# Typed neighbour sums on one core: two nodes per counting slot, counts as bytes of 16-bit integers, and 480 counted chunks instead of 464

## The chip, the cores and the metric

The kernel runs on 1 core of one Trainium2 chip. A core has TensorE (PE, matrix products into PSUM; PEld in the profile is its weight load), VectorE (DVE), ScalarE (ACT), GpSimd (POOL) and SyncE (SP, which here only issues DMAs). The metric is the device time in microseconds, the median of the runs shown; lower is better. Before the change it is 1467.21 us (3 runs, 1465.16 to 1470.11).

## The reference

There are 12,500 nodes with 128 features, and 200,000 edges with a source node, a destination node and one of 4 types. The edges are sorted by destination, and the destinations are drawn as 12500 u² with u uniform, so that low nodes have many edges and high nodes few.

```
h = relu(layernorm(x))                      # 12500 x 128
msgs = sum_i where(type == i, h[src] @ W[i] + b[i], 0)    # 200000 x 128
out = x + segment_sum(msgs, dst, 12500)
```

The sum over edges can be taken before the product with W: for every destination and every type, add up the rows h[src], multiply the four sums by the four W, and add each b as often as its type occurs.

## The kernel before

The 200,000 edges are 1563 chunks of 128. A constant, C0 = 464, splits them. The first C0 chunks (destinations with many edges) go the counted way, the other TM = 1099 the gathered way. Both run at once in one program order.

*The node table.* In the first eight groups of chunks (RAW = 8) the kernel also normalises all nodes and writes h to DRAM (`htab`) as three bf16 parts whose sum is h. These groups gather rows of x itself; later ones gather rows of `htab`.

*The gathered way.* A group has G = 16 chunks; the last four groups have 12, 8, 4 and 3. For each chunk POOL issues one indirect DMA (L403) that fetches 128 rows. DVE makes a one-hot of destination and type (L424), PE sums the rows with it (L461, three products for the three parts), ACT evicts the sums (L468), PE multiplies them by W (L475), and DVE adds the result into a ring of destinations (L487). Buffers `hm` hold 5 x 8 chunks, so POOL can be 40 chunks ahead of PE. When destinations are complete, `put_out` takes four tiles of 128 nodes from the ring, PE transposes them (L509), DVE adds x (L512) and SP writes them out.

*The counted way.* For the first ND destinations the kernel doesn't fetch rows. It counts, for each destination, how many of its edges come from each source with each type, and multiplies `htab` by the counts. A *slot* is a column of up to 128 edges of one destination; `make_slots` builds the slots in the head of the kernel: `loT` and `hkT` hold, for each edge of a slot, the source's low part (0 to 127) and its high part combined with the type (1 to 392, 0 for none). A destination with over 128 edges has several slots, its levels; two levels share a *virtual* node. `count` makes two one-hots per slot on DVE (L737 with 128 columns, L738 with 392), multiplies them on PE (L742: a 128 x 392 table of counts in PSUM, a second level being added to the first), and ACT evicts the table of each virtual node as one byte of fp8 per count into `counts` (L745), with the sum of each row as accumulator output (`both`), which serves a check of the largest count. `multiply` then takes a batch of up to 92 virtual nodes (VBMAX), loads `htab` with 25 DMAs on SP (L763, `hs`, 5 buffers), and runs 98 x 3 products of 128 x 128 with up to 368 columns of counts (L766) into one PSUM tile, `pa`. It is evicted (L776), multiplied by W (L779) and added to `acc` (L784).

*The order.* `dense_work` is a generator that alternates the counting of one batch with the multiplication of the batch before it, in step with the share of each that is done. `pace` spreads it over the groups: it counts PE columns, and lets each group from RAW to `last` have the same sum of gathered and counted columns. The place of each instruction in its engine's queue is therefore fixed when the program is built; the engines meet through semaphores. After `last`, what is left of the counted work is issued at once, then come the remaining groups and the output of `acc`. At the end `check_all` sums the checks; if `flag` is set, a slow loop computes everything again.

With C0 = 464 there are ND = 1144 counted destinations, 1336 slots and 1180 virtual nodes in 15 batches (23, 46, eleven of 92, 53, 46), and 67 full groups.

Of the kernel before, what the change touches and what calls it, by code (L numbers as in the profile page):

```python
# [31 lines left out]
F32 = mybir.dt.float32  # L35
BF16 = mybir.dt.bfloat16
F16 = mybir.dt.float16
F8 = mybir.dt.float8e4
I32 = mybir.dt.int32
AF = mybir.ActivationFunctionType  # L40
ALU = mybir.AluOpType
AX = mybir.AxisListType
# [4 lines left out]
P = 128  # L47
# [4 lines left out]
WIN = 32  # L52
RAW = 8
ROOM = 12
C0 = 464
VBMAX = 92
MANY = 16
HB = 4
# [9 lines left out]
def kernel(  # L68
# [47 lines left out]
    virtual = [(k, d) for k in range(0, len(levels), 2) for d in range(levels[k])]  # L116

    virtual = virtual[ND - 2 * VBMAX : ND] + virtual[: ND - 2 * VBMAX] + virtual[ND:]
    VB = VBMAX
    sizes_of = [VB // 4, VB // 2]  # L120
    left = len(virtual) - sum(sizes_of) - VB // 2
    sizes_of += [VB] * (left // VB) + ([left % VB] if left % VB else []) + [VB // 2]
    batches = [virtual[sum(sizes_of[:i]) :][:n] for i, n in enumerate(sizes_of)]
    NB = NW * NT


# [427 lines left out]
    def check_all():  # L554

        low = const.tile([P, BM], F32, name="low")
        step = const.tile([P, BM], F32, name="step")
        nc.vector.memset(low, 0.0)
        for (ja, jb, _), i in zip(flushes, goes):
            if starts[i] + sizes[i] < TM:  # L560
                nc.vector.tensor_scalar(
                    step, rowf, starts[i] + sizes[i] - 0.5, (jb - ja) * float(P), ALU.is_gt, ALU.mult
                )
                nc.vector.tensor_add(low, low, step)
        bad = const.tile([P, 5], F32, name="bad")
# [10 lines left out]
        many = const.tile([P, 2], F32, name="many")  # L576
        nc.vector.tensor_reduce(many[:, 0:1], bad, AX.X, ALU.add)
        nc.vector.tensor_copy(many[:, 1:2], seen)
        pb = x_ps.tile([P, 2], F32, name="pt")
        nc.tensor.matmul(pb, ones, many, start=True, stop=True)  # L580
        sums_ok = const.tile([P, 2], F32, name="sums_ok")
        nc.vector.tensor_single_scalar(sums_ok[:, 0:1], pb[:, 0:1], 0.5, op=ALU.is_gt)
        nc.vector.tensor_single_scalar(sums_ok[:, 1:2], pb[:, 1:2], 3.0 * E0, op=ALU.not_equal)
        nc.vector.tensor_reduce(flag, sums_ok, AX.X, ALU.max)


# [12 lines left out]
    def make_slots(dix):  # L599
# [79 lines left out]
        def unpack(a, z):  # L679
            n = z - a  # L680
            hk = dix.tile([P, 512], I32, name="hk")
            nc.vector.tensor_single_scalar(hk[:, :n], packed[:, a:z], 7, op=ALU.arith_shift_right)
            nc.vector.tensor_copy(hkT[:, a:z], hk[:, :n])
            nc.vector.scalar_tensor_tensor(
                loT[:, a:z], hkT[:, a:z], float(-P), packed[:, a:z], op0=ALU.mult, op1=ALU.add
            )

            nc.vector.tensor_single_scalar(hk[:, :n], hk[:, :n], NT - 1, op=ALU.bitwise_and)
            ohs = []
            for t in range(NT):  # L690
                is_t = dix.tile([P, 512], BF16, name="is_t", bufs=NT)
# [32 lines left out]

    def count(vs, counts):
        todo = []
        for i, (k, d) in enumerate(vs):
            todo.append((i, starts_of[k] + d, True, not (k + 1 < len(levels) and d < levels[k + 1])))
            if not todo[-1][3]:
                todo.append((i, starts_of[k + 1] + d, False, True))  # L730
        both = sdp.tile([P, VB], F32, name="both", bufs=2)
        for s0 in range(0, len(todo), OB):
            part = todo[s0 : s0 + OB]
            o1 = ohp.tile([P, OB, P], BF16, name="o1")
            o2 = ohp.tile([P, OB, NB], BF16, name="o2")
            for k, (i, s, first, last) in enumerate(part):
                nc.vector.tensor_scalar(o1[:, k, :], iota_b, loT[:, s : s + 1], None, ALU.is_equal)  # L737
                nc.vector.tensor_scalar(o2[:, k, :], iota_n, hkT[:, s : s + 1], None, ALU.is_equal)  # L738
            for k, (i, s, first, last) in enumerate(part):
                if first:  # L740
                    pb = x_ps.tile([P, NB], F32, name="pt")
                nc.tensor.matmul(pb, o1[:, k, :], o2[:, k, :], start=first, stop=last)  # L742
                if last:

                    nc.scalar.activation(  # L745
                        counts[:, :, i * NT : (i + 1) * NT],
                        pb.rearrange("p (b t) -> p b t", t=NT),
                        AF.Copy,
                        accum_out=both[:, i : i + 1],
                        saturate=True,  # L750
                    )
                yield (s0 + k + 1) / len(todo)
        top = sdp.tile([P, 1], F32, name="top")
        nc.vector.tensor_reduce(top, both[:, : len(vs)], AX.X, ALU.max)
        nc.vector.tensor_max(most, most, top)

    def multiply(vs, counts):
        nv = len(vs)
        pa = a_ps.tile([P, VB * NT], F32, name="pa")
        for j0 in range(0, NW, HB):  # L760
            j1 = min(j0 + HB, NW)
# [10 lines left out]
                    )  # L772
            if j1 < NW:
                yield j1 / NW
        sd = sdp.tile([P, VB, NT], F32, name="sd")
        nc.scalar.copy(sd[:, :nv].rearrange("p v t -> p (v t)"), pa[:, : nv * NT])  # L776
        py = y_ps.tile([P, VB], F32, name="py")
        for t in range(NT):
            nc.tensor.matmul(py[:, :nv], wsb[:, t, :], sd[:, :nv, t], start=(t == 0), stop=(t == NT - 1))  # L779
        i = 0  # L780
        while i < nv:
            k, d = vs[i]
            n = next((m for m in range(1, nv - i) if vs[i + m] != (k, d + m)), nv - i)
            nc.vector.tensor_tensor(acc[:, d : d + n], acc[:, d : d + n], py[:, i : i + n], ALU.add)  # L784
# [7 lines left out]

    def pace(gi, part):

        last = FULL - 2
        if gi >= last:
            return 2.0
        own = [columns(i) for i in range(RAW, last)]
# [2 lines left out]
        return ((n + part) * a_group - sum(own[:n]) - part * own[n]) / dense_columns()  # L801

    def dense_columns():
        return NS * float(NB) + len(virtual) * NW * 3.0 * NT

    def dense_work():

# [5 lines left out]
        for vs in batches + [None]:  # L813
            steps = {}
            now = None
            if vs:
                now = vs, dense.tile([P, NW, VB * NT], F8, name="counts")
                slots = sum(1 + (k + 1 < len(levels) and d < levels[k + 1]) for k, d in vs)
                steps[count(*now)] = slots * a_slot
# [12 lines left out]
            before = now  # L832

    seen = const.tile([P, 1], F32, name="seen")
    slots = mid.enter_context(tc.tile_pool(name="slots", bufs=1, side="right"))
    loT = slots.tile([P, NS], F32, name="loT")
    hkT = slots.tile([P, NS], F32, name="hkT")
    building = ExitStack()
    dix = building.enter_context(tc.tile_pool(name="dix", bufs=1, side="right"))
    to_slots = make_slots(dix)  # L840
# [5 lines left out]
    for gi, (t0, g) in enumerate(zip(starts, sizes)):  # L846
# [85 lines left out]
        if gi == RAW - 1:  # L932
# [11 lines left out]
            most = sdp.tile([P, 1], F32, name="most")  # L944
            nc.vector.memset(most, 0.0)
            work = dense_work()
        for (ja, jb, _), i in zip(flushes, goes):
            if i == gi:
# [135 lines left out]
```

## Time and profile before

| | before |
|---|---|
| median of 3 runs | 1467.21 us |
| the profiled execution, its time / span | 1466.72 / 1465.0 us |
| granted TensorE clock, mean | 0.95 |
| PE, weight load busy | 1305.8, 866.6 us |
| DVE, ACT, POOL busy | 1055.8, 860.7, 1078.9 us |
| DMA | 282.11 MB, mean 193 GB/s |
| gathers: from `htab`, from x | 971, 128 |

Busy time is the union of the times in which an engine had an instruction in work. Instructions on PE, DVE and ACT overlap their successors, so the mean duration of one is longer than its share of the engine; the trace also has every start, and start-to-start times tell what one costs. A line of a group of instructions gives line, engine, operation, output <- inputs, shapes and count, then busy time and mean ns of one, then the idle time of the engine just before them with what ended it. A line of waits gives the engine and line that waited, what ended the wait, the total in us, how many, and the longest. A line of the chain of waits gives start, length, and what.

### The profile page before, as it was taken

To read this page: it belongs to the slowest core of one execution; us is meant where nothing else is said; L and a number is where in the kernel's file an instruction comes from. 1 tells how busy PE (TensorE), PEld (TensorE's weight loads), DVE (VectorE), ACT (ScalarE), POOL (GpSimd) and SP (SyncE) were. 2 spreads that over 40 slices of the span, in tenths; PEclk is the share of its full clock that TensorE was granted. 3 is DMA by queue.
4 is the path that set the end of the run, shared out by engine and by line. 5 is a ranking of instruction groups with operands and counts; after the bars stand their busy time and mean duration, and the time that the engine had idled before them with its cause. 6 is when DMAs were issued, how large, how long until landed. Compare 5 with 4: busy or idle time off the path is not lost.

```text
span 1465.0 us, 32946 instructions
## 1 busy us (share of the span) xinstructions
PE 1305.8 (89%) x10222; PEld 866.6 (59%) x10222; DVE 1055.8 (72%) x5728; ACT 860.7 (59%) x3026; POOL 1078.9 (74%) x1109
## 2 busy tenths in 40 slices
PE   1566787998999999999999999999999999999964
PEld 0444455765666556666666666666666666677743
DVE  8796878879889877677675786757787676677233
ACT  7776447867545566566655666646766665445010
POOL 7777775677677767777777777777777777777773
PEclk9995768999999999999999999999999999999977
DMA  7643247975566567676676767776676667777841
GB/s 214 181 138 115 89 149 245 299 231 173 154 193 176 165 183 204 190 225 200 202 205 196 210 186 207 199 200 201 192 209 193 190 194 212 216 237 252 304 121 54
DMA packets 141833, 282.11 MB, mean 193 GB/s; under 512 B 26995, under 2 KB 74661, under 8 KB 141653
## 3 DMA queue, kind: packets, MB, share of 16 engines
q1 hardware_dynamic: 90949, 176.07, 38.3%
q0 software_dynamic: 50704, 103.91, 26.3%
q8 instruction: 80, 1.31, 0.3%
q14 instruction: 100, 0.82, 0.2%
HBM read 263.84 MB, written 16.03 MB: 191 GB/s over the span
## 4 chain that ended last, share of the span: by engine, by line
PE 70%; DVE 11%; ACT 4%; DMA 3%; POOL 2%; issue 2%; DVEq 0%; ACTq 0%; POOLq 0%
PE pa L766 35%; PE pt L742 13%; PE py L475 9%; PE ps L461 8%; ACT counts L745 3%; DVE o L738 3%; DVE o L737 2%; POOL hm L403 2%; DVE ring L487 2%; DMA hs<-htab 2%; DVE oh L424 2%; DMA hm<-htab,srcT 1%; PE ps L444 1%; PE ps L446 1%; PE py L779 1%
## 5 line engine op out<-in xcount | busy, mean ns | idle before, releaser
L403 POOL DMA_INDIRECT hm<-htab,srcT x971 | 947.0, 975 | 322.4 <-issue 266.9
L766 PE MATMUL pa<-counts,hs 128*128 128x368 fp8e4 (+3 forms) x4410 | 713.2, 299 | 7.2 <-DMA hs<-htab 6.4
L745 ACT ACTIVATE counts<-pt 128x392 fp8e4<-128x392 f32 x1180 | 574.7, 519 | 169.7 <-PE pt L742 165.8
L766 PEld LDWEIGHTS <-hs 128*128 128x128 bf16 x4410 | 404.3, 99 | 232.4 <-issue 31.7
L738 DVE TENSOR_SCALAR o<-iota_n,hkT 128x392 bf16<-128x392 f16 x1336 | 450.3, 337 | 0.0
L737 DVE TENSOR_SCALAR o<-iota_b,loT 128x128 bf16<-128x128 bf16 x1336 | 346.8, 260 | 128.5 <-PE pt L742 126.7
L742 PE MATMUL pt<-o,o 128*128 128x392 bf16 x1336 | 368.0, 333 | 11.4 <-ACT counts L745 3.9
L745 ACT ACTIVATION_READ_ACCUMULATOR counts<-pt 128x1 f32 x1180 | 268.7, 228 | 0.0
L487 DVE TENSOR_TENSOR ring<-ring,py 128x16 f32 (+4 forms) x1072 | 187.3, 175 | 106.8 <-PE py L475 89.8
L468 ACT COPY sb<-ps 128x320 f32<-128x320 f32 (+4 forms) x275 | 115.8, 424 | 234.1 <-PE ps L461 210.0
L424 DVE TENSOR_SCALAR oh<-iota_b,keyT 128x64 bf16<-128x64 bf16 (+4 forms) x971 | 179.2, 265 | 90.1 <-PE ps L461 88.2
L461 PE MATMUL ps<-oh,hm 128*128 128x80 bf16 (+4 forms) x2913 | 160.0, 202 | 20.9 <-DMA hm<-htab,srcT 19.8
L461 PEld LDWEIGHTS <-hm 128*128 128x128 bf16 x2913 | 136.8, 99 | 59.1 <-DMA hm<-htab,srcT 26.2
L742 PEld LDWEIGHTS <-o 128*128 128x128 bf16 x1336 | 125.5, 99 | 78.0 <-DVE o L738 13.0
L475 PE MATMUL py<-sb,wsb 128*128 128x384 f32 (+4 forms) x536 | 170.9, 454 | 0.3 <-ACT sb L468 0.3
L403 POOL DMA_INDIRECT hm<-in_x_dram,srcT x128 | 130.4, 1019 | 40.8 <-issue 36.9
L475 PEld LDWEIGHTS py<-sb,wsb 128*128 128x128 f32 x536 | 107.0, 211 | 38.3 <-issue 13.7
L450 ACT CAST cnt<-ps 128x256 bf16<-128x256 f32 (+7 forms) x71 | 29.3, 413 | 130.0 <-PE ps L446 112.4
L461 PE MATMUL ps<-ohf,hm 128*128 128x48 f32 x256 | 59.0, 391 | 51.5 <-ACT hm L365 51.5
L461 PEld LDWEIGHTS ps<-ohf,hm 128*128 128x128 f32 x256 | 52.8, 298 | 69.0 <-ACT hm L365 55.7
L365 ACT ACTIVATE hm<-hm,nmr,rstd 128x128 f32<-128x128 f32 x128 | 51.0, 481 | 6.3 <-DVE nmr L356 6.3
L473 PE MATMUL py<-cnt,b 128*128 128x256 bf16 (+5 forms) x67 | 20.7, 309 | 24.0 <-DVE ring L487 22.8
(173 smaller groups left out, 551.7 us busy)
## 6 DMA issues: line engine op xcount, KB each, us to landing
hs<-htab SPq DMA_DIRECT2D x360, 384.0 KB
hm<-htab,srcT POOLq DMA_INDIRECT x971
htab<-h SPq DMA_DIRECT2D x11, 768.0 KB
xo<-in_x_dram SPq DMA_DIRECT2D x23, 256.0 KB
out_dram<-xo SPq DMA_DIRECT2D x23, 256.0 KB
xt<-in_x_dram SPq DMA_DIRECT2D x6, 512.0 KB
hs<-htab SPq DMA_DIRECT2D x15, 192.0 KB
xt<-in_x_dram SPq DMA_DIRECT2D x5, 448.0 KB
```

What stands on the lines that cost most here:

```text
L365: nc.scalar.activation(h(k), xt(k), AF.Relu, bias=nmr[:r, k : k + 1], scale=rstd[:r, k : k + 1])
L403: nc.gpsimd.indirect_dma_start(out=rows[:, (i - h0) * width : (i - h0 + 1) * width], out_offset=None, in_=table, in_offset=bass.IndirectOf ...
L424: nc.vector.tensor_scalar(oh[:, i, :], (iota_f if raw else iota_b)[:, :K], keyf[:, t0 + i : t0 + i + 1], None, ALU.is_equal)
L461: mm = nc.tensor.matmul(ps[:, i - i0, :], rows(i, c, nparts), oh[:, i, :], start=(c == 0), stop=(c == nparts - 1),)
L468: nc.scalar.copy(sb[:, i0:i1].rearrange("p g t n -> p g (t n)"), ps[:, : i1 - i0, :])
L475: mm = nc.tensor.matmul(py[:, :g, :], wsb[:, t, :], sb[:, :g, t, :], start=False, stop=(t == NT - 1))
L487: nc.vector.tensor_tensor(to, to, py[:, i, :], ALU.add)
L737: nc.vector.tensor_scalar(o1[:, k, :], iota_b, loT[:, s : s + 1], None, ALU.is_equal)
L738: nc.vector.tensor_scalar(o2[:, k, :], iota_n, hkT[:, s : s + 1], None, ALU.is_equal)
L742: nc.tensor.matmul(pb, o1[:, k, :], o2[:, k, :], start=first, stop=last)
L745: nc.scalar.activation(counts[:, :, i * NT : (i + 1) * NT], pb.rearrange("p (b t) -> p b t", t=NT), AF.Copy, accum_out=both[:, i : i + 1], ...
L766: nc.tensor.matmul(pa[:, : nv * NT], hs[:, j - j0, c * D : (c + 1) * D], counts[:, j, : nv * NT], start=(j == 0 and c == 0), stop=(j == NW ...
```

## The change

Line numbers in the new kernel are 37 to 68 higher (L403 is L440, L742 is L791, L745 is L794, L766 is L826).

1. *Pairs.* `count` works on units of two virtual nodes. The second node's one-hot of the low part is multiplied by 256, so that one PSUM table holds n1 + 256 n2. Its eviction writes 16-bit unsigned integers, and `multiply` reads the same bytes as fp8, two per integer. As raw fp8 bytes the counts 0 to 16 stand for themselves over 512, and the eviction of `pa` has scale 512.
2. *Shared slots.* From destination PAIRS = 558 on, two neighbours have few enough edges that both fit one slot. `make_slots` adds the second's `loT` and `hkT` onto the first's (an edge row of one is zero where the other has one), and `byT` holds the factor, 1 or 256, for each edge.
3. *480 chunks.* C0 = 480: 1083 gathered chunks and 66 full groups. `last` is FULL - 1 instead of FULL - 2, which is group 65 in both. ND = 1224; 1260 places for virtual nodes (630 units) in 16 batches (22, 46, twelve of 92, 42, 46); 1083 slots to count. Batches mix paired and shared nodes in proportion.
4. *Checks.* Per batch, `both` is split into its two bytes for the largest count, and summed into `held`, which must come to the number of counted edges.

```diff
-C0 = 464
+C0 = 480
...
+    PAIRS = next(
+        d
+        for d in range(levels[1] + levels[1] % 2, ND, 2)
+        if (lambda m: m + 6 * m**0.5)(E * (((d + 2) / N) ** 0.5 - (d / N) ** 0.5)) <= P
+    )
+    alone = [(k, d) for k in range(0, len(levels), 2) for d in range(min(levels[k], PAIRS))]
+    if len(alone) % 2:
+        alone.append(None)
+    shared = [(0, d) for d in range(PAIRS, ND)]
...
+    def slots_of(u):
+        if u[0] is not None and u[0][0] == 0 and u[0][1] >= PAIRS:
+            return [(u[0][1], None)]
+        got = []
+        for v, by in zip(u, (1.0, 256.0)):
+            if v is not None:
+                k, d = v
+                got.append((starts_of[k] + d, by))
+                if k + 1 < len(levels) and d < levels[k + 1]:
+                    got.append((starts_of[k + 1] + d, by))
+        return got
...
+        one, two = slice(PAIRS, ND, 2), slice(PAIRS + 1, ND, 2)
+        nc.vector.tensor_scalar(byT, hkT[:, two], 0.5, 255.0, ALU.is_gt, ALU.mult)
+        nc.vector.tensor_single_scalar(byT, byT, 1.0, op=ALU.add)
+        for of in (loT, hkT):
+            nc.vector.tensor_tensor(of[:, one], of[:, one], of[:, two], ALU.add)
...
-                nc.vector.tensor_scalar(o1[:, k, :], iota_b, loT[:, s : s + 1], None, ALU.is_equal)
+                if by == 1.0:
+                    nc.vector.tensor_scalar(o1[:, k, :], iota_b, loT[:, s : s + 1], None, ALU.is_equal)
+                else:
+                    if by is None:
+                        by = byT[:, (s - PAIRS) // 2 : (s - PAIRS) // 2 + 1]
+                    nc.vector.tensor_scalar(o1[:, k, :], iota_b, loT[:, s : s + 1], by, ALU.is_equal, ALU.mult)
                 nc.vector.tensor_scalar(o2[:, k, :], iota_n, hkT[:, s : s + 1], None, ALU.is_equal)
...
                         AF.Copy,
                         accum_out=both[:, i : i + 1],
-                        saturate=True,
                     )
...
-        top = sdp.tile([P, 1], F32, name="top")
-        nc.vector.tensor_reduce(top, both[:, : len(vs)], AX.X, ALU.max)
-        nc.vector.tensor_max(most, most, top)
+        n = len(vs) // 2
+        bi = sdp.tile([P, VB // 2], I32, name="bi")
+        nc.vector.tensor_copy(bi[:, :n], both[:, :n])
+        bb = sdp.tile([P, 2, VB // 2], I32, name="bb")
+        nc.vector.tensor_single_scalar(bb[:, 0, :n], bi[:, :n], 255, op=ALU.bitwise_and)
+        nc.vector.tensor_single_scalar(bb[:, 1, :n], bi[:, :n], 8, op=ALU.arith_shift_right)
+        bf = sdp.tile([P, 2, VB // 2], F32, name="bf")
+        nc.vector.tensor_copy(bf[:, :, :n], bb[:, :, :n])
+        top = sdp.tile([P, 2], F32, name="top")
+        nc.vector.tensor_reduce(top[:, 0:1], bf[:, :, :n], AX.XY, ALU.max)
+        nc.vector.tensor_reduce(top[:, 1:2], bf[:, :, :n], AX.XY, ALU.add)
+        nc.vector.tensor_max(most, most, top[:, 0:1])
+        nc.vector.tensor_add(held, held, top[:, 1:2])
...
+        counts = counts.bitcast(F8)
...
-        nc.scalar.copy(sd[:, :nv].rearrange("p v t -> p (v t)"), pa[:, : nv * NT])
+        sd = sdp.tile([P, VB // 2, NT, 2], F32, name="sd")
+        nc.scalar.activation(
+            sd[:, : nv // 2].rearrange("p v t m -> p (v t m)"), pa[:, : nv * NT], AF.Copy, scale=512.0
+        )
...
-        last = FULL - 2
+        last = FULL - 1
...
-                now = vs, dense.tile([P, NW, VB * NT], F8, name="counts")
+                now = vs, dense.tile([P, NW, VB // 2 * NT], U16, name="counts")
```

More of the change, by code (lines that the diff above doesn't have):

```diff
@@ L39 @@
 I32 = mybir.dt.int32
+U16 = mybir.dt.uint16
 AF = mybir.ActivationFunctionType
@@ L115, with units @@
     NDT = -(-ND // P)
-    virtual = [(k, d) for k in range(0, len(levels), 2) for d in range(levels[k])]
-    virtual = virtual[ND - 2 * VBMAX : ND] + virtual[: ND - 2 * VBMAX] + virtual[ND:]
-    VB = VBMAX
[L120 to L123, printed above, removed]
+    PAIRS = next(
[7 more added lines that the diff above has]
+    shared = [(0, d) for d in range(PAIRS, ND)]
+    VB = VBMAX
+    sizes_of = [VB // 8 * 2, VB // 4 * 2]
+    left = len(alone) + len(shared) - sum(sizes_of) - VB // 4 * 2
+    sizes_of += [VB] * (left // VB) + ([left % VB] if left % VB else []) + [VB // 4 * 2]
+    batches = []
+    a = b0 = 0
+    for i, n in enumerate(sizes_of):
+        na, ns = len(alone) - a, len(shared) - b0
+        n1 = 0 if i < 2 else min(round(n * na / (na + ns) / 2) * 2, na)
+        n1 = max(n1, n - ns)
+        batches.append(alone[a : a + n1] + shared[b0 : b0 + n - n1])
+        a, b0 = a + n1, b0 + n - n1
+    assert a == len(alone) and b0 == len(shared)
+    def slots_of(u):
[9 more added lines that the diff above has]
+        return got
+    def units(vs):
+        return [tuple(vs[i : i + 2]) for i in range(0, len(vs), 2)]
+    NSLOTS = sum(len(slots_of(u)) for vs in batches for u in units(vs))
     NB = NW * NT
@@ L575, in check_all @@
         nc.vector.tensor_single_scalar(bad[:, 4:5], most, MANY + 0.5, op=ALU.is_gt)
-        many = const.tile([P, 2], F32, name="many")
+        many = const.tile([P, 3], F32, name="many")
         nc.vector.tensor_reduce(many[:, 0:1], bad, AX.X, ALU.add)
         nc.vector.tensor_copy(many[:, 1:2], seen)
-        pb = x_ps.tile([P, 2], F32, name="pt")
+        nc.vector.tensor_copy(many[:, 2:3], held)
+        pb = x_ps.tile([P, 3], F32, name="pt")
         nc.tensor.matmul(pb, ones, many, start=True, stop=True)
-        sums_ok = const.tile([P, 2], F32, name="sums_ok")
+        sums_ok = const.tile([P, 3], F32, name="sums_ok")
         nc.vector.tensor_single_scalar(sums_ok[:, 0:1], pb[:, 0:1], 0.5, op=ALU.is_gt)
         nc.vector.tensor_single_scalar(sums_ok[:, 1:2], pb[:, 1:2], 3.0 * E0, op=ALU.not_equal)
+        nc.vector.tensor_single_scalar(sums_ok[:, 2:3], pb[:, 2:3], float(E0), op=ALU.not_equal)
         nc.vector.tensor_reduce(flag, sums_ok, AX.X, ALU.max)
@@ L690, in unpack @@
             for t in range(NT):
-                is_t = dix.tile([P, 512], BF16, name="is_t", bufs=NT)
+                is_t = dix.tile([P, 512], BF16, name="sel", bufs=2 * DENSE)
                 if t < NT - 1:
@@ L726, in count @@
         todo = []
[L727 to L731, printed above, removed]
+        for i, u in enumerate(units(vs)):
+            of = slots_of(u)
+            todo += [(i, c, by, n == 0, n == len(of) - 1) for n, (c, by) in enumerate(of)]
+        both = sdp.tile([P, VB // 2], F32, name="both", bufs=2)
         for s0 in range(0, len(todo), OB):
@@ L735, in count @@
             o2 = ohp.tile([P, OB, NB], BF16, name="o2")
-            for k, (i, s, first, last) in enumerate(part):
-                nc.vector.tensor_scalar(o1[:, k, :], iota_b, loT[:, s : s + 1], None, ALU.is_equal)
+            for k, (i, s, by, first, last) in enumerate(part):
+                if by == 1.0:
[4 more added lines that the diff above has]
+                    nc.vector.tensor_scalar(o1[:, k, :], iota_b, loT[:, s : s + 1], by, ALU.is_equal, ALU.mult)
                 nc.vector.tensor_scalar(o2[:, k, :], iota_n, hkT[:, s : s + 1], None, ALU.is_equal)
-            for k, (i, s, first, last) in enumerate(part):
+            for k, (i, s, by, first, last) in enumerate(part):
                 if first:
@@ L774, in multiply @@
                 yield j1 / NW
-        sd = sdp.tile([P, VB, NT], F32, name="sd")
-        nc.scalar.copy(sd[:, :nv].rearrange("p v t -> p (v t)"), pa[:, : nv * NT])
+        sd = sdp.tile([P, VB // 2, NT, 2], F32, name="sd")
+        nc.scalar.activation(
+            sd[:, : nv // 2].rearrange("p v t m -> p (v t m)"), pa[:, : nv * NT], AF.Copy, scale=512.0
+        )
         py = y_ps.tile([P, VB], F32, name="py")
         for t in range(NT):
-            nc.tensor.matmul(py[:, :nv], wsb[:, t, :], sd[:, :nv, t], start=(t == 0), stop=(t == NT - 1))
+            nc.tensor.matmul(py[:, :nv].rearrange("p (v m) -> p v m", m=2), wsb[:, t, :], sd[:, : nv // 2, t, :], start=(t == 0), stop=(t == NT - 1))
         i = 0
         while i < nv:
+            if vs[i] is None:
+                i += 1
+                continue
             k, d = vs[i]
@@ L803, in dense_columns @@
     def dense_columns():
-        return NS * float(NB) + len(virtual) * NW * 3.0 * NT
+        return NSLOTS * float(NB) + sum(len(vs) for vs in batches) * NW * 3.0 * NT
     def dense_work():
@@ L816, in dense_work @@
             if vs:
-                now = vs, dense.tile([P, NW, VB * NT], F8, name="counts")
-                slots = sum(1 + (k + 1 < len(levels) and d < levels[k + 1]) for k, d in vs)
-                steps[count(*now)] = slots * a_slot
+                now = vs, dense.tile([P, NW, VB // 2 * NT], U16, name="counts")
+                steps[count(*now)] = sum(len(slots_of(u)) for u in units(vs)) * a_slot
             if before:
@@ L834 @@
     seen = const.tile([P, 1], F32, name="seen")
+    most = const.tile([P, 1], F32, name="most")
+    held = const.tile([P, 1], F32, name="held")
+    for t in (most, held):
+        nc.vector.memset(t, 0.0)
     slots = mid.enter_context(tc.tile_pool(name="slots", bufs=1, side="right"))
@@ L837 @@
     hkT = slots.tile([P, NS], F32, name="hkT")
+    byT = slots.tile([P, (ND - PAIRS) // 2], F32, name="byT")
     building = ExitStack()
@@ L943 @@
             hsp = mid.enter_context(tc.tile_pool(name="hsp", bufs=5))
-            most = sdp.tile([P, 1], F32, name="most")
-            nc.vector.memset(most, 0.0)
             work = dense_work()
```

## The prediction

> **What bounds the kernel now.** I read the page first, its totals and costliest groups, to see who is loaded and how many instructions of each kind there are.
>
> ```profile
> PE 1305.8 (89%) x10222; PEld 866.6 (59%) x10222; DVE 1055.8 (72%) x5728; ACT 860.7 (59%) x3026; POOL 1078.9 (74%) x1109
> ...
> L403 POOL DMA_INDIRECT hm<-htab,srcT x971 | 947.0, 975 | 322.4 <-issue 266.9
> L766 PE MATMUL pa<-counts,hs 128*128 128x368 fp8e4 (+3 forms) x4410 | 713.2, 299 | 7.2 <-DMA hs<-htab 6.4
> L745 ACT ACTIVATE counts<-pt 128x392 fp8e4<-128x392 f32 x1180 | 574.7, 519 | 169.7 <-PE pt L742 165.8
> ...
> L738 DVE TENSOR_SCALAR o<-iota_n,hkT 128x392 bf16<-128x392 f16 x1336 | 450.3, 337 | 0.0
> L737 DVE TENSOR_SCALAR o<-iota_b,loT 128x128 bf16<-128x128 bf16 x1336 | 346.8, 260 | 128.5 <-PE pt L742 126.7
> L742 PE MATMUL pt<-o,o 128*128 128x392 bf16 x1336 | 368.0, 333 | 11.4 <-ACT counts L745 3.9
> ```
>
> TensorE looks like the only bound. But POOL's 74% hides something: the time between its gathers is nearly all "issue". Next I read POOL's own waits.
>
> ```profile
> POOL hm L403 <- issue: 303.8, 997, 0.3
> POOL hm L403 <- PE pt L742: 21.7, 33, 6.6
> POOL hm L403 <- PE ps L461: 16.2, 11, 12.4
> POOL hm L403 <- PE pa L766: 8.0, 21, 1.9
> ```
>
> 997 of 1099 gathers follow their predecessor after a fixed 0.305 us (303.8 / 997); with the median gather of 0.946 us that is 1.251 us from start to start, and the trace's starts have that median. Only some 50 us in the run are waits for a buffer. So POOL has a hard pace: 16 chunks in 20.02 us. The table by stretches (columns: length, then busy time and count for PE, PEld, DVE, ACT, POOL, the clock, DMA) shows where it is held.
>
> ```profile
> 240.00:260.00 20.00, 15.97 (x223) 12.01 (x222) 15.67 (x72) 12.06 (x48) 6.11 (x6) 0.85 0.96 324
> 260.00:300.00 40.00, 37.98 (x419) 30.10 (x416) 34.28 (x189) 36.21 (x147) 29.52 (x30) 1.00 0.89 294
> 300.00:400.00 100.00, 92.74 (x793) 60.93 (x792) 85.41 (x468) 64.03 (x243) 70.94 (x71) 0.98 0.62 183
> 600.00:800.00 200.00, 196.75 (x1563) 126.90 (x1560) 142.67 (x792) 129.27 (x495) 152.45 (x157) 1.00 0.70 203
> 1400.00:1420.00 20.00, 12.74 (x78) 7.60 (x76) 6.75 (x36) 2.45 (x6) 15.13 (x17) 0.66 0.35 95
> ```
>
> At 1.251 us a gather, 20 us hold 16, 100 us 80, 200 us 160. POOL does 6 in 240 to 260 (DMA 96% busy), 71 in 300 to 400, but 157 in 600 to 800, its pace less some jitter. Summing start-to-start times over 1.251 us in the trace: 11.8 us before 230, 12.7 in 230 to 260, 25.9 in 260 to 600, 13.8 after; 64.2 in all. Check: 4.1 (first gather) + 1098 x 1.251 + 64.2 = 1441.9, the start of the last. In 1400 to 1420 PE is 64% busy while POOL issues without a pause: the tail waits for gathers. Last I read the chain of waits.
>
> ```profile
> 329.93 10.73 ACT counts L745 x44
> ...
> 1433.12 2.56 DMA hm<-htab,srcT
> 1435.72 0.47 PE ps L461 x3
> ...
> 1456.73 0.64 PE pt L509 x4
> ```
>
> Early on there are stretches where only counting runs, at the speed of the evictions; at the end, the gather of the last chunk of the 8-chunk group (start 1433.1), then 32 us of small groups and output. So POOL sets the end, and PE runs close behind it: in 600 to 1300 the lag from a chunk's gather to its first matmul falls from 37 us (chunk 600) to 20 (chunk 1000). Both must get shorter for the kernel to gain.
>
> **The change part by part.** Busy means overstate pipelined instructions, so I price by start-to-start times from the trace (25th percentile): L742 0.1655 us, L766 0.1555 at 368 columns (0.091, 0.079, 0.040 at 212, 184, 92), L737 0.162, L738 0.231, an eviction 0.377 plus its accumulator read 0.093.
>
> *Sixteen gathers go.* TM falls from 1099 to 1083 and full groups from 67 to 66. 16 x 1.251 = 20.0 us off POOL's path. On PE that group is 48 L461, 8 L475 and the small ones, about 4.7 us; on DVE 6.5. The interleaving still ends with group 64 (the two edits to `last` and FULL cancel), so 43 instead of 59 chunks follow the counted work.
>
> *Counting.* One-hots and L742 fall from 1336 to 1083 slots although 80 more nodes are counted: PE 253 x 0.1655 = -41.9 us, DVE 253 x 0.393 = -99 us. Evictions fall from 1180 to 630: ACT 550 x 0.470 = -259 us. The wider 16-bit output I cost at nothing: L776 writes 368 f32 columns in 0.345 us, L745 392 one-byte columns in 0.377, the same per column.
>
> *Two operations in one one-hot* (708 of the 1083 L737). Nearest row: the two-operation L636, 112 columns in 0.098 us and 1007 in 0.332, as fast per column as L738. Lower bound nothing; upper, if a second per-partition scalar cost the fast mode, the 1.02 ns per column of L665 (0.600 us at 512, 0.200 at 120), about +0.1 us each, 71 us of DVE. I take nothing, the row.
>
> *Multiplying.* 1260 instead of 1180 nodes means 16 batches: L766 summed over batches goes from 294 x (11 x 0.1555 + 0.091 + 2 x 0.079 + 0.040) = 588 to 628 us: +40, and 25 more hs loads of 384 KB on SP and DMA (9.6 MB, at 203 GB/s with a DMA share of 0.70 there is room after 300 us). The new per-batch checks are about 0.7 us more DVE per batch (eight small ones of 0.07 to 0.17 us, the rows L754 and L755), 11 us in all, beside PE. The added scale is inside the eviction of `pa`. Before the dense stage, byT and the two in-place sums are four DVE instructions on 333 columns and the last pieces are 80 columns wider: about 2.5 us, and this sits on the path (L695, L700, L714 lie in the chain at 197 to 202). I count it in full.
>
> *Balance per stage.* PE over all is -41.9 + 40.1 - 4.7, so its work per paced group is unchanged, some 19.2 us against POOL's 20.0. What changes is DVE and ACT: two batches of before have 161 and 160 slots: 161 x 0.393 + 5.1 groups x 6.5 = 96 us of DVE where POOL wants 102, with stalls whenever they bunch. After, the heaviest large batches have 115: 75 us of 92; the rest 69: 53 of 81, ACT 30 of 81. So of the 25.9 us held in 260 to 600 I keep the later jitter, 13.8 / 890 x 340 = 5, plus 4 for batch 2 (DVE 64 us of 59): 9. The 230 to 260 stall stays: 96% busy DMA, and the first multiply needs its 25 hs loads however few nodes it has. It is now earlier by 12 evictions (about 6 us) but with 10 more loads in group 8 (3.9 MB at 324 GB/s, 12 us): between -6 and +6, taken as 0, plus the 2.5.
>
> *Sum.* Last gather: 4.1 + 1082 x 1.251 + (11.8 + 12.7 + 2.5 + 9 + 13.8 = 49.8) = 1407.5; then 23.1 as before (1465.0 - 1441.9): span 1430.6. The profiled run was 1466.7 for a span of 1465.0, the median 1467.2, so +2: **1432 us**, 2.4% less.
>
> PE must follow. From 264 to 1391, 1127 us, it needed 1063 us for dense work and groups and 10 for output transposes: 54 us of waits. After: 1080. From the end of the dense work 7.4 us of group 65, some 10 of the 12-chunk group and the 29.3 from 1435.7 to the end are left, 47 in all, so it may end at 1384: 40 us of waits may stay. With 23% fewer slots and half the evictions I estimate 35. This is the tight place.
>
> *Two rules weighed.* The row of L403 has a median of 0.946 us, minimum 0.940, amid 2672 fast one-hots. The Trainium skill, "SBUF — State Buffer", section "Who interferes with whom", says a two-port VectorE copy or tensor_scalar locks GpSimd out for its whole length, so fewer one-hots would free the gathers. By the rule a share 253/1336 of all waits after 600, about 3 us, would go; by the row nothing. I take the row. The second speaks against the change. The clock in the rows above is 1.00 while PE works and 0.66 in the tail. "TensorE: Matmul & The Clock Gate", "Part 1: The HAM clock gate", says that about 3.4 us of idleness halves the clock. If PE now waits for each group's gathers, it idles about 0.9 us in 20, and the longest such wait in the trace before the tail is about 2 us: no penalty. By the rule, a full window idle in each of the last ten groups would cost 10 x 1.7 = 17 us of PE.
>
> **The rivals.** *A: the stalls return elsewhere.* The DMA-bound start and bunched counting hold POOL for the same 64 us and only the gathers go: 1465.0 - 20.0 + 2 = 1447. For it: PE's total work hardly falls. Against it: the runs of L742 at 0.39 and 0.48 us in 310 to 530 are exactly DVE's and ACT's paces.
>
> *B: PE becomes the end.* All 54 us of waits stay and the start is 4 us late: 268 + 1080 + 54 + 47 + 2 = 1451, to 1460 with colder tails. For it: 99% busy PE in 600 to 1300. Against: the waits are mostly for DVE and ACT.
>
> *C, slower: DVE falls behind.* If the two-operation one-hot costs far more than its row, DVE sets the 69-slot batches: they take 53 + 46 c, c the extra of each of their 46 two-operation one-hots. That passes POOL's 81 us at c = 0.61 us, and the kernel is slower than before once twelve large batches lose 35 us, 3 each: c = 0.67. At c = 0.8 they lose 12 x 9 = 108 us: 1540. Nothing in the trace has such a price: even the slow bound is 0.1.
>
> *D: the change doesn't do what it says.* If the new test of `held` raises the flag, the fallback loop of 1563 turns follows; with a single gather in each turn, 1563 x 0.946 is 1.5 ms more. Counts up to 16 are the same integers read as raw bytes times 512, so I see no reason.
>
> **How the numbers follow.** Forecast 0.65 (own range 1418 to 1445), A 0.13, B 0.12, C 0.06, D 0.04. About 0.3% is what a measurement tells from no change, so 1463 to 1471 is "same": a quarter of B, 0.03. Slower is C and D, 0.10; faster 0.87. For the range I leave out C, D, the upper half of B and the lowest few in a hundred of the forecast: 1417 to 1453, which holds A and both bounds of the start.
>
> **What would show it.** Right: 1083 gathers at 1.251 us, 76 or more in 300 to 400, evictions x630 near 519 ns, ACT under 45%, L766 x4704, last gather near 1407. The steps fail if L737's two-operation form is longer than 260 ns by a tenth of a us, if POOL's waits for PE stay at 50 us, or if the dense work ends after 1384 while gathers are long done. Wrong altogether: POOL waiting in 600 to 1300, which would mean that PE, not POOL, had set the pace.

## The result, and the profile after

The changed kernel takes 1441.9 us (median of 4 runs, 1440.01 to 1443.55) against 1466.18 us for the kernel before (now 4 runs, 1462.83 to 1470.11). The ratio is 0.9833, with a 95% interval of 0.9804 to 0.9862: 1.7% faster. The forecast was 1432 us with a range of 1417 to 1453. The profiled execution took 1440.69 us for a span of 1439.0.

The page of the changed kernel first, its totals and groups; L440, L826, L794, L787, L782 with L786, and L791 are the former L403, L766, L745, L738, L737 and L742.

```profile
PE 1274.2 (89%) x10210; PEld 857.0 (60%) x10210; DVE 982.2 (68%) x5310; ACT 598.0 (42%) x1922; POOL 1059.0 (74%) x1093
...
L440 POOL DMA_INDIRECT hm<-htab,srcT x955 | 925.2, 969 | 313.5 <-issue 267.5
L826 PE MATMUL pa<-counts,hs 128*128 128x368 fp8e4 (+3 forms) x4704 | 715.7, 298 | 14.4 <-DMA hs<-htab 13.1
...
L794 ACT ACTIVATE counts<-pt 128x392 uint16<-128x392 f32 x630 | 309.4, 504 | 279.1 <-PE pt L791 275.7
L787 DVE TENSOR_SCALAR o<-iota_n,hkT 128x392 bf16<-128x392 f16 x1083 | 359.5, 332 | 0.0
L791 PE MATMUL pt<-o,o 128*128 128x392 bf16 x1083 | 278.9, 334 | 6.6 <-ACT counts L794 2.5
...
L782 DVE TENSOR_SCALAR o<-iota_b,loT 128x128 bf16<-128x128 bf16 x375 | 99.1, 264 | 88.5 <-PE pt L791 87.8
L786 DVE TENSOR_SCALAR o<-iota_b,loT,byT 128x128 bf16<-128x128 bf16 x333 | 110.9, 333 | 40.6 <-PE pt L791 40.1
...
L786 DVE TENSOR_SCALAR o<-iota_b,loT 128x128 bf16<-128x128 bf16 x375 | 95.9, 256 | 1.3 <-PE pt L791 1.2
```

Read the counts: 550 evictions and 253 slots are gone, 294 products have come. ACT is at 42%. The 16-bit eviction costs what the 8-bit one did (504 and 519 ns). PE's share is 89% before and after, and yet the kernel is faster. POOL's own waits and the stretches tell more (columns as before).

```profile
POOL hm L440 <- issue: 303.4, 996, 0.3
POOL hm L440 <- PE ps L498: 23.7, 10, 10.8
POOL hm L440 <- PE pt L791: 8.9, 22, 2.2
```

```profile
240.00:260.00 20.00, 14.78 (x245) 11.22 (x245) 12.43 (x67) 5.67 (x22) 15.26 (x16) 1.00 1.02 365
260.00:300.00 40.00, 37.16 (x400) 30.28 (x399) 38.00 (x214) 13.07 (x45) 22.84 (x22) 1.00 0.82 274
300.00:400.00 100.00, 94.82 (x783) 61.13 (x782) 84.67 (x458) 41.80 (x156) 70.49 (x70) 0.98 0.64 195
600.00:800.00 200.00, 196.89 (x1571) 128.05 (x1570) 126.36 (x698) 82.41 (x295) 151.68 (x159) 0.99 0.70 212
1400.00:1420.00 20.00, 13.76 (x78) 8.41 (x79) 6.07 (x28) 1.70 (x5) 11.34 (x12) 0.78 0.39 112
```

POOL's pace is the old one: a median of 1.251 us from start to start. In 600 to 800 it issues 159 gathers where 160 fit; before it was 157. The early stall has moved: 16 gathers in 240 to 260, where there had been 6, but 22 instead of 30 in 260 to 300, and 70 in the next 100 us, where there had been 71. Adding start-to-start times over 1.251 us as in the prediction:

| stretch | before | forecast | after |
|---|---|---|---|
| to 230 us | 11.8 | 14.3 | 14.4 |
| 230 to 600 | 38.6 | 21.7 | 29.9 |
| after 600 | 13.8 | 13.8 | 12.0 |
| sum | 64.2 | 49.8 | 56.3 |
| last gather starts | 1441.9 | 1407.5 | 1413.9 |
| from there to the end | 23.1 | 23.1 | 25.1 |

So of the 26.0 us that the span lost, 20.0 are the 16 gathers at POOL's pace, 8 are shorter stalls, and 2 went back in the tail. That is arithmetic on two traces. The page's own chain of waits seems to say something else:

```profile
PE 67%; DVE 8%; DMA 6%; POOL 6%; issue 3%; ACT 3%; DVEq 0%; SPq 0%; ACTq 0%; POOLq 0%
```

It gives PE two thirds, because PE and POOL release each other all the time, and the chain follows a release even when it came within POOL's usual 0.3 us (20 of the 22 waits for L791 above are such). Which engine sets the end is what the experiments ask.

### The profile page after: what moved, and what is told of

Same layout as the page of the kernel before. It is cut to its first block, busy times and chain, and to the rows that moved or that the text cites. A ratio compares the mean times of both kernels' runs of the same rounds, so it can differ in the third digit from the quotient of the medians.

```text
span 1439.0 us, 31409 instructions
## 1 busy us (share of the span) xinstructions
PE 1274.2 (89%) x10210; PEld 857.0 (60%) x10210; DVE 982.2 (68%) x5310; ACT 598.0 (42%) x1922; POOL 1059.0 (74%) x1093
## 4 chain that ended last, share of the span: by engine, by line
PE 67%; DVE 8%; DMA 6%; POOL 6%; issue 3%; ACT 3%; DVEq 0%; SPq 0%; ACTq 0%; POOLq 0%
PE pa L826 36%; PE pt L791 10%; PE py L512 8%; PE ps L498 7%; POOL hm L440 6%; DMA hs<-htab 3%; ACT counts L794 2%; DVE ring L524 2%; DVE o L787 2%; DMA hm<-htab,srcT 1%; DVE o L786 1%; DVE oh L461 1%; PE ps L481 1%; PE py L841 1%; PE ps L483 1%
## 5 line engine op out<-in xcount | busy, mean ns | idle before, releaser
L440 POOL DMA_INDIRECT hm<-htab,srcT x955 | 925.2, 969 | 313.5 <-issue 267.5
L826 PE MATMUL pa<-counts,hs 128*128 128x368 fp8e4 (+3 forms) x4704 | 715.7, 298 | 14.4 <-DMA hs<-htab 13.1
L826 PEld LDWEIGHTS <-hs 128*128 128x128 bf16 x4704 | 427.8, 98 | 239.1 <-DMA hs<-htab 20.2
L794 ACT ACTIVATE counts<-pt 128x392 uint16<-128x392 f32 x630 | 309.4, 504 | 279.1 <-PE pt L791 275.7
L787 DVE TENSOR_SCALAR o<-iota_n,hkT 128x392 bf16<-128x392 f16 x1083 | 359.5, 332 | 0.0
L791 PE MATMUL pt<-o,o 128*128 128x392 bf16 x1083 | 278.9, 334 | 6.6 <-ACT counts L794 2.5
L505 ACT COPY sb<-ps 128x256 f32<-128x256 f32 (+5 forms) x271 | 111.8, 417 | 311.8 <-PE ps L498 276.7
L498 PE MATMUL ps<-oh,hm 128*128 128x64 bf16 (+4 forms) x2865 | 154.3, 202 | 29.5 <-DMA hm<-htab,srcT 29.1
L498 PEld LDWEIGHTS <-hm 128*128 128x128 bf16 x2865 | 131.5, 99 | 64.2 <-DMA hm<-htab,srcT 36.0
L512 PE MATMUL py<-sb,wsb 128*128 128x384 f32 (+4 forms) x528 | 164.5, 452 | 0.0
L440 POOL DMA_INDIRECT hm<-in_x_dram,srcT x128 | 132.3, 1033 | 41.8 <-issue 36.0
L782 DVE TENSOR_SCALAR o<-iota_b,loT 128x128 bf16<-128x128 bf16 x375 | 99.1, 264 | 88.5 <-PE pt L791 87.8
L786 DVE TENSOR_SCALAR o<-iota_b,loT,byT 128x128 bf16<-128x128 bf16 x333 | 110.9, 333 | 40.6 <-PE pt L791 40.1
L791 PEld LDWEIGHTS <-o 128*128 128x128 bf16 x1083 | 100.4, 99 | 56.3 <-DVE o L787 10.9
L794 ACT ACTIVATION_READ_ACCUMULATOR counts<-pt 128x1 f32 x630 | 131.9, 209 | 0.0
L512 PEld LDWEIGHTS py<-sb,wsb 128*128 128x128 f32 x528 | 105.8, 211 | 35.2 <-issue 9.9
L498 PE MATMUL ps<-ohf,hm 128*128 128x48 f32 x256 | 59.1, 385 | 52.9 <-ACT hm L402 52.9
L786 DVE TENSOR_SCALAR o<-iota_b,loT 128x128 bf16<-128x128 bf16 x375 | 95.9, 256 | 1.3 <-PE pt L791 1.2
L498 PEld LDWEIGHTS ps<-ohf,hm 128*128 128x128 f32 x256 | 52.1, 291 | 71.7 <-ACT hm L402 59.1
```

The lines of the kernel that those rows point to most:

```text
L440: nc.gpsimd.indirect_dma_start(out=rows[:, (i - h0) * width : (i - h0 + 1) * width], out_offset=None, in_=table, in_offset=bass.IndirectOf ...
L498: mm = nc.tensor.matmul(ps[:, i - i0, :], rows(i, c, nparts), oh[:, i, :], start=(c == 0), stop=(c == nparts - 1),)
L505: nc.scalar.copy(sb[:, i0:i1].rearrange("p g t n -> p g (t n)"), ps[:, : i1 - i0, :])
L512: mm = nc.tensor.matmul(py[:, :g, :], wsb[:, t, :], sb[:, :g, t, :], start=False, stop=(t == NT - 1))
L794: nc.scalar.activation(counts[:, :, i * NT : (i + 1) * NT], pb.rearrange("p (b t) -> p b t", t=NT), AF.Copy, accum_out=both[:, i : i + 1],)
L826: nc.tensor.matmul(pa[:, : nv * NT], hs[:, j - j0, c * D : (c + 1) * D], counts[:, j, : nv * NT], start=(j == 0 and c == 0), stop=(j == NW ...
```

## The experiments

The theory: POOL's gathers set the end, PE is just behind. Rival A: only the gathers count, since what pairing saves is lost in stalls elsewhere. Rival B: PE sets the end.

One thing has to be known before the times are read. Only one of the runs below, the first, met a chip like that of the result, with the kernel before at 1470.82 us. On five other chips every kernel took about half as long again, the kernel before too (2167 to 2221 us); of those "slower chips" I give ratios to the kernel before on the same chip, and read them apart. The changed kernel itself was not run on one of them.

### A third of the counted product left out

```diff
             for j in range(j0, j1):
-                for c in range(3):
+                for c in range(2):
                     nc.tensor.matmul(
                         pa[:, : nv * NT],
...
-                        stop=(j == NW - 1 and c == 2),
+                        stop=(j == NW - 1 and c == 1),
```

> The changed kernel without the third bf16 part of h in the counted product (two of three products of L826 are left, so part of the result's precision is left out), once more. On a chip where the kernel before is near 1466 us: the theory (POOL's gathers set the end, PE is just behind) says 1418 to 1437 us; rival B (PE sets the end) under 1380 us. Where the kernel before is near 2170 us: about 0.91 of it.

Measured: 1446.18 us in one run, beside 1470.82 for the kernel before on that chip: 0.983 of it, as the changed kernel. PE has 1568 products less, some 200 us of work, and the kernel is not faster than the changed one; its own span is 5.4 us longer (1444.4 against 1439.0). POOL's waits in it, and the stretches:

```profile
POOL hm L440 <- issue: 308.3, 1012, 0.3
POOL hm L440 <- PE ps L498: 19.5, 9, 11.4
```

```profile
260.00:300.00 40.00, 33.76 (x292) 25.89 (x291) 33.58 (x189) 12.48 (x45) 22.22 (x23) 0.88 0.81 263
300.00:400.00 100.00, 88.23 (x703) 55.14 (x702) 84.03 (x450) 41.89 (x157) 68.86 (x70) 0.89 0.68 203
600.00:800.00 200.00, 162.79 (x1267) 103.08 (x1266) 121.70 (x693) 80.40 (x282) 151.87 (x159) 0.90 0.67 202
1400.00:1420.00 20.00, 11.53 (x58) 6.22 (x58) 4.16 (x24) 1.31 (x3) 12.02 (x13) 0.59 0.27 69
```

PE falls from 197 to 163 busy us in 600 to 800, and POOL issues 159 gathers as in the changed kernel. The last gather starts at 1414.7, against 1413.9. What PE no longer has to do it spends waiting for gathers; these are its waits in the kernel before, the changed kernel and this one:

```profile
PE ps L461 <- DMA hm<-htab,srcT: 19.8, 22, 2.1
PE ps L498 <- DMA hm<-htab,srcT: 29.1, 31, 2.0
PE ps L498 <- DMA hm<-htab,srcT: 136.1, 155, 2.6
```

Rival B is refuted for this chip: if PE set the end, most of the 200 us would show. My own range, 1418 to 1437, was missed too, and the trace shows two places. First, the stalls of POOL at 260 to 400 are all there with a third less product work, so the counted product's work on PE is not their cause. Second, the end comes 29.7 us after the last gather instead of 25.1, with a clock of 0.59 instead of 0.78 in 1400 to 1420; that the clock makes the difference is likely and not shown.

On a slower chip the same kernel was run beside the others:

> The changed kernel without the third bf16 part of h in the counted product (two of three products of L826 are left, so part of the result's precision is left out), which takes some 200 us of work from PE; the gathers and the loads are the same. Theory (POOL sets the end, PE is just behind): 1083 x 1.251 and the stalls of the head stay, 1418 to 1437 us, 5 to 24 less than the changed kernel. Rival B (PE sets the end): a loss of 200 us of PE work shows for the most part, under 1380 us.

Measured there: 0.9113 of the kernel before (0.9046 to 0.918).

### The pairs alone, with 464 chunks

```diff
-C0 = 480
+C0 = 464
```

> The new counting with C0 = 464, so 1099 gathers as before, 1043 slots, 590 evictions, 15 batches. Theory (POOL's gathers at 1.251 us set the end): the 16 gathers come back and nothing else, 16 x 1.251 = 20 us over the changed kernel, 1455 to 1464 us, although PE has some 42 us less matrix work than in the changed kernel. Rival B (PE sets the end): PE's smaller work shows, 1400 to 1425 us. Rival A (what the pairs win is lost to stalls): as the kernel before, 1464 to 1470.

> The new counting with C0 = 464 once more, because in the first call every kernel, the one before too, took about half as long again, with idle time on every engine that no record accounts for. On a chip where the kernel before is near 1466 us: the theory (POOL's gathers set the end) says 1455 to 1464 us, 20 us over the changed kernel; rival B (PE sets the end) 1400 to 1425 us; rival A 1464 to 1470 us. If the kernel before is near 2170 us again: about 0.925 of it.

> The new counting with C0 = 464: 1099 gathers, 1043 slots, 590 evictions, 15 batches. Theory (POOL's gathers set the end): 20 us over the changed kernel, 1455 to 1464 us, although PE has some 42 us less matrix work. Rival B (PE sets the end): 1400 to 1425 us. Rival A (the pairs win nothing of their own, their room goes to stalls elsewhere): 1464 to 1470 us.

Measured, on three slower chips: 0.9254 (0.9202 to 0.9307), 0.9275 (0.9224 to 0.9325) and 0.9297 (0.9245 to 0.9348). There the pairs alone bring some 7%, far more than the whole change brings on the faster chip. The ranges in us were meant for the faster chip, so none of them is tested. The profile shows in what the chips differ. Of the second of these runs, first the chain by engine, then waits of POOL, then those of PE's weight loads:

```profile
PE 50%; another core or an unknown queue 20%; DVE 13%; issue 10%; ACT 4%; DMA 1%; POOL 1%; DVEq 0%; SPq 0%; ACTq 0%; POOLq 0%
```

```profile
POOL hm L440 <- PE ps L498: 323.9, 51, 28.3
POOL hm L440 <- issue: 294.7, 965, 0.6
POOL hm L440 <- PE pt L791: 251.3, 39, 31.6
```

```profile
PEld L826 <- issue: 214.3, 654, 5.7
PEld L498 <- issue: 152.9, 195, 10.6
PEld L791 <- issue: 93.1, 120, 11.6
```

Single instructions are as fast as before (L826 0.156 us from start to start where it runs on, gathers 1.251), but PE idles for hundreds of us without a releaser in the records, and POOL waits for PE: 324 + 251 us, against 24 + 9 in the changed kernel on the faster chip. Between chunks 300 and 1000 a gather comes every 1.78 us. So POOL's pace no longer sets the end there. Why the engines idle stays open, and the traces help less than they seem to: after 300 us PE, DVE and ACT all stand idle at once for 322 us (20 in the kernel before on the faster chip), and of 4069 DVE instructions that signal its semaphore only 2784 have the signal on record (4500 of 4596 there). A wait without a releaser can be a hole in the record.

### The old counting with 480 chunks

The kernel before with this one edit:

```diff
-C0 = 464
+C0 = 480
```

> The old counting, one slot per node, with C0 = 480: 1083 gathers, 1416 slots, 1260 evictions, 16 batches. Theory: PE gets 80 x 0.1655 + 40 = 53 us of work more and passes POOL, so the end is PE's: 264 + 1126 + 54 of waits + 47 + 2 = about 1493, between 1480 and 1505 us. If gathers alone counted, and PE had room in plenty: 1447 us.

> The old counting, one slot per node, with C0 = 480: 1083 gathers, 1416 slots, 1260 evictions, 16 batches. Theory: PE, with 53 us of work more, passes POOL and sets the end: 1480 to 1505 us. If gathers alone counted: 1447 us.

Measured, on a slower chip: 1.0466 (1.0403 to 1.053), and on another 2302.93 us beside 2221.29 (1.037) in one run. With POOL waiting for PE, 16 gathers less bring nothing that shows, and 53 us more of PE's work, with the evictions that go with it, costs 82 to 105 us. The sign is the theory's for a kernel in which PE sets the end, but the range in us is not tested, nor what the gathers alone are worth on the faster chip.

### Pairs without shared slots

Every node keeps a slot of its own; only the table and its eviction are shared. The large destinations come later in the order, as in the kernel before.

```diff
-    PAIRS = next(
-        d
-        for d in range(levels[1] + levels[1] % 2, ND, 2)
-        if (lambda m: m + 6 * m**0.5)(E * (((d + 2) / N) ** 0.5 - (d / N) ** 0.5)) <= P
-    )
+    PAIRS = ND
     alone = [(k, d) for k in range(0, len(levels), 2) for d in range(min(levels[k], PAIRS))]
+    alone = alone[ND - 2 * VBMAX : ND] + alone[: ND - 2 * VBMAX] + alone[ND:]
...
-        one, two = slice(PAIRS, ND, 2), slice(PAIRS + 1, ND, 2)
-        nc.vector.tensor_scalar(byT, hkT[:, two], 0.5, 255.0, ALU.is_gt, ALU.mult)
-        nc.vector.tensor_single_scalar(byT, byT, 1.0, op=ALU.add)
-        for of in (loT, hkT):
-            nc.vector.tensor_tensor(of[:, one], of[:, one], of[:, two], ALU.add)
...
```

> The changed kernel with pairs, 16-bit evictions and C0 = 480, but no slot shared: 1416 slots for 630 evictions; the large destinations come later in the order, as in the kernel before. Theory: the shared slots are what makes room on PE (333 x 0.1655 = 55 us) and the halved evictions only lessen waits, so this is PE-bound like the old counting with 480 chunks, at most 20 us better: 1470 to 1500 us. Rival (ACT's evictions were what held PE): 1440 to 1450 us.

> The changed kernel with pairs, 16-bit evictions and C0 = 480, but no slot shared: 1416 slots for 630 evictions. Theory: the shared slots are what makes room on PE (333 x 0.1655 = 55 us), the halved evictions only lessen waits: 1465 to 1495 us. Rival (ACT's evictions were what held PE): 1440 to 1450 us.

Measured, on the same two slower chips: 0.949 (0.9434 to 0.9547), and 2115.39 beside 2221.29 us (0.952) in one run. It has the slots, gathers and products of the old counting with 480 chunks, which took 1.0466 and 1.037. So where POOL waits for PE, two nodes to a table and half the evictions, 630 instead of 1260, are worth 8 to 9% (2061 against 2274 us, 2115 against 2303), and I had given them 20 us at most. PE's own waits for ACT before a counting product say part of why; of the old counting, then of this one:

```profile
PE pt L742 <- ACT counts L745: 139.5, 64, 13.5
PE pt L781 <- ACT counts L784: 42.0, 16, 8.6
```

That is some 100 of the 213 us; for most of the rest the records name nobody (the two kernels also differ in the checks and in `last`). For the faster chip this says nothing, as POOL hides it.

### Another start

```diff
-    sizes_of = [VB // 8 * 2, VB // 4 * 2]
+    sizes_of = [VB // 4 * 2]
```

> The changed kernel with batches of 46, 92, ... instead of 22, 46, 92, ...: 15 passes over htab, not 16 (25 loads, 9.6 MB, fewer), the first pass spread over some two groups instead of one, and the second counted batch made of shared slots alone (46 slots, not 115). PE's matrix work is the same to 2 us. Theory: what still holds POOL after the head, 24 us between 260 and 350 us, is the DMA-bound first pass and DVE's bunched one-hots of the 115-slot batch, not PE; so this takes 10 to 20 us off, 1422 to 1432 us. Rival: the stall belongs to the change from raw to table rows itself; unchanged, 1439 to 1444 us.

> The changed kernel with batches of 46, 92, ... instead of 22, 46, 92, ...: 15 passes over htab instead of 16, the first pass spread over two groups, the second counted batch of 46 shared slots. Theory: the 24 us that hold POOL between 260 and 350 us in the changed kernel, which stayed when a third of the counted product was left out, come from the DMA-bound first pass and DVE's one-hots for the 115-slot batch: 1422 to 1432 us where the kernel before is near 1466. Rival: the stall belongs to the change from raw to table rows itself; 1439 to 1444 us.

> The changed kernel with batches of 46, 92, ... instead of 22, 46, 92, ...: 15 passes over htab instead of 16, the first spread over two groups, the second counted batch of 46 shared slots. Theory: the 24 us that hold POOL between 260 and 350 us in the changed kernel, which stayed when a third of the counted product was left out, come from the DMA-bound first pass and DVE's one-hots for the 115-slot batch: 1422 to 1432 us where the kernel before is near 1466. Rival: the stall belongs to the change from raw to table rows itself; 1439 to 1444 us. Where the kernel before is near 2170 us: about 0.915 of it.

Measured, on three slower chips: 0.9164 (0.9112 to 0.9216), 1980.89 beside 2166.97 us (0.914) in one run, and 0.9151 (0.9082 to 0.922). POOL gets from chunk 160 to chunk 232 in 151 to 153 us, against 162 us in the kernel with two parts, which has the changed kernel's batches; but by chunk 300 that lead has shrunk or gone (271 to 284 us from chunk 160, against 286). As the changed kernel was not run on those chips, whether this is better or worse than it is not known, and whether it takes the stall away on the faster chip is not shown. This remains the next thing to try.

## Why the prediction was right, point by point

*POOL's pace sets the end.* Right. The gathers' spacing is unchanged, 1083 were issued, the time between chunks 300 and 1000 fell to 1.271 us a gather from 1.283, and with 200 us less of PE's work the last gather started 0.8 us later and PE waited 136 us for gathers. The 20.0 us for the sixteen gathers are the largest part of the gain. A run with the gathers alone changed, on the faster chip, is missing; their share is read from the traces.

*The head, +2.5 us.* Right: 14.4 measured to 230 us, 14.3 forecast.

*The stalls from 230 to 600.* This is the term that was mis-sized: 21.7 forecast, 29.9 measured. One of the prediction's own signs failed with it: 70 gathers in 300 to 400, where 76 or more were to show it. The start of the counted work I took as "0 between -6 and +6", and it was: a stall of 10.6 us at 268 us, in place of one of 12.2 at 245. The DMA engines are busy all the time in 240 to 260 (a share of 1.02 in the table), while group 8 loads all 25 pieces of the first pass. The error is the end of batch 2. I set its DVE work (64 us for a place of 59) at 4 us of stall; it is 8.4 us in one piece at 323, and 10.7 in 300 to 350. The order of time there:

```profile
317.61 3.90 PE L826 MATMUL pa<-counts,hs 128*128 128x368 fp8e4 x24
321.35 1.14 PE L512 MATMUL py<-sb,wsb 128*128 128x192 f32 x6
322.53 0.17 DVE L524 TENSOR_TENSOR ring<-ring,py 128x12 f32 x1 [3.42 <-PE py L512]
326.46 0.27 PE L483 MATMUL ps<-oh,three 128*32 128x192 bf16 x4 [3.97 <-DVE oh L461]
331.59 0.46 PE L498 MATMUL ps<-oh,hm 128*128 128x48 bf16 x12
332.32 0.94 POOL L440 DMA_INDIRECT hm<-htab,srcT  x1 [8.72 <-PE ps L498]
```

DVE is not too slow here: it stands idle for 3.42 us, waiting for a group's products (L512), which stand in PE's queue behind 24 products of the next batch. Then PE stands idle for 3.97 us, waiting for the next group's one-hots, which DVE makes in turn with the additions into the ring. After this pause the granted clock is halved:

```profile
326.60:330.00 3.40, 3.40 (x26) 1.85 (x23) 3.04 (x15) 1.21 (x4) 0.00 (x0) 0.50 0.01 2
```

Only then does L498 free POOL's buffer. The balance by batch found the place, but what it priced, a surplus of DVE's work, is not what held POOL: two in-order queues waited for each other, and the clock added to it (an estimate: at most 1.7 us, half of these 3.4). From 350 to 600 the stalls are 5.4 us, as the forecast jitter of 5 for 340 us, although two more batches of 115 slots lie there.

*The two-operation one-hot.* I took nothing, with an upper bound of 0.1 us. With 256 as a constant it is nothing: 0.162 us from start to start, as with one operation. With the factor as a second per-partition operand it is 0.223, so +0.061 us for 333 of them, 20 us of DVE over the run. It lies beside PE, but 23 of batch 2's 115 slots have it, 1.4 us of its excess. Rival C needed ten times that.

*PE must follow.* It did, but with nothing to spare: the last L826 starts at 1384.9, where 1384 was the limit and about 1379 the estimate, and the gathers ran 6.4 us late themselves. After 600 POOL waits longer than its 0.3 us once, for 1.9 us. The estimate that PE's waits would fall was wrong: counted as time without a matmul from 264 us to the end of the dense work, they are 31 us before and 40 after, since PE now waits for gathers. (The 1080 us of work in the prediction are not the sum of the parts it shows, 1063 + 10 - 41.9 + 40.1 = 1071; the trace has PE busy for 1081.)

*The tail*, 25.1 instead of 23.1 us, I had carried over. The chain of the changed kernel near the end:

```profile
1377.09 6.40 DMA hs<-htab
...
1402.69 2.58 DMA hm<-htab,srcT
1405.27 0.05 issue
1405.32 0.28 PE ps L498
...
1415.51 2.19 DMA out_dram<-xo
1417.71 3.88 DMA xo<-in_x_dram
```

A gather of the 8-chunk group is in the chain as before, its sixth and not its last. Then an output buffer `xo` has to be written out and read in again before DVE can go on, 6 us that were not in the chain of before. With one group fewer after the counted work, the outputs of `acc` probably meet the last groups; no run shows it, and the kernel with two parts has no such wait in its chain and a longer tail.

*The two rules.* Of the Trainium skill's "SBUF — State Buffer", section "Who interferes with whom", I took nothing, by the row's median of 0.946 us. The median hides it. I compared the lengths of all gathers after 600 us with what DVE does meanwhile:

| mean length of a gather, us | before | after |
|---|---|---|
| beside no 392-column one-hot (L738, L787) | 0.946 (301) | 0.946 (337) |
| beside one | 0.984 (361) | 0.979 (305) |
| sum over 0.946 | 13.8 | 9.9 |

More than half of the gathers beside such a one-hot keep their length, and some are longer by 0.1 us and more. The 13.8 us that I carried over as jitter are all of this kind, and 9.9 of the 12.0 after; the rest is the one wait of 1.9 us. So the 3 us that the rule gave were about right (3.9), and my "nothing" was wrong. That the one-hots cause it is read from two traces; no run changed them alone.

"TensorE: Matmul & The Clock Gate" I had set at nothing, as no wait for gathers would last 3.4 us. That was wrong in its reasoning. Already in the kernel before the clock fell for 3.4 us at 365 and 492, after pauses of 4.3 and 3.1 us for a group's one-hots, and at 526 and 1355, with no pause over 1 us in the 10 us ahead. In the changed kernel, near 890 us, PE had caught up with POOL and took one chunk at a time:

```profile
880.00:890.00 10.00, 5.90 (x76) 4.08 (x73) 2.77 (x17) 2.81 (x8) 7.56 (x9) 0.99 0.38 116
886.40:889.80 3.40, 1.42 (x15) 0.77 (x13) 0.17 (x1) 0.77 (x3) 2.48 (x4) 1.00 0.26 71
890.00:900.00 10.00, 3.44 (x28) 1.68 (x28) 4.09 (x32) 0.64 (x2) 7.56 (x9) 0.50 0.29 80
```

No pause of PE was over 1.0 us in the 10 us before, none over 1.8 us after, and the clock still went to a half, for 20.5 us in one piece; in the kernel before no such piece after 270 us was over 3.4 us until the tail. POOL was not held by it there, because PE had time; the half clock at 326 us was part of the stall above.

*The sum of the 9.9 us* between 1432 and 1441.9: the last gather 6.4 late (8.2 more in 230 to 600, 1.8 less after), tail 2.0, 0.9 because the median lies 2.9 above the span and not 2, and 0.6 because 1432.6 was written as 1432. Rival A, at 1447, was nearer to the result than the forecast, by its number: what pairing won in stalls is 8 us, between A's nothing and the 14 forecast. The range of 1417 to 1453 held both, so its being right does not tell them apart; the starts of the gathers do.

## What to carry to other kernels

Look for an engine whose instructions follow each other at a fixed distance with nothing in between: POOL's busy share of 74% was its full speed, and taking work from PE at 89% gave no time back. When a change moves the balance of such a pair, sum the time over the fixed pace by stretches, before and after: it shows where the gain stays and where it goes back. Before a stall is put down to the busiest engine, read it in the order of time: the 8.4 us at 323 began with DVE idle. And look behind a median: 178 of the 662 gathers after 600 us were over 0.02 us longer than the median in the kernel before, and they held all of the 13.8 us.

## What the runs showed of the hardware that I had not expected

- TensorE's clock was halved for 20.5 us although no pause of PE was over 1.0 us in the 10 us before: in the last 3.4 us ahead of it PE was busy for 1.42 us. A low share of work was enough, no long pause was needed.
- A gather that POOL issues beside a 392-column one-hot on DVE takes 0.033 to 0.038 us more on average (0.979 and 0.984 us, against 0.946), while its median hardly moves.
- A tensor_scalar on 128 bf16 columns costs 0.162 us from start to start with one operation, or with two of which the second has a constant, and 0.223 us when the second operand is a column of per-partition values too.
- The same kernel can take 1.5 times as long on another chip, with unchanged start-to-start times of single instructions and idle time on PE that no record explains, and there the same edits have other values: 7% for the pairs alone, and 8 to 9% between the kernels with 480 chunks for two nodes to a table.
